# Where the inner rows of one batch are computed: after the attention, or beside the attention of the other batch

## The chip, the cores and the metric

One core of one Trainium2 chip runs the whole program. The metric is the device time of an execution in microseconds (us); several executions are timed, and one more is recorded by the hardware profiler. TensorE (PE) multiplies matrices and writes its sums into PSUM banks; ScalarE (ACT), VectorE (DVE) and GpSimd (POOL) read and write SBUF and PSUM; SyncE (SP) and ACT issue transfers between DRAM and SBUF on queues. Each engine runs its own list of instructions in order and waits on semaphores for the others.

## The reference

One transformer block in fp32, with batch 2, 1024 tokens, width 1024, 32 heads of 32 and an inner width of 2752. Cut to what matters:

```python
mod = (silu(c) @ wmod).reshape(2, 6, 1, -1)          # 1024 x 6144
sa, ca, ga, sb, cb, gb = ...                         # ga, gb kept away from zero
h = layernorm(x) * (1 + ca) + sa
qkv = clip(h @ Wqkv.T, -8, 8); q = layernorm(q); k = layernorm(k)
p = softmax(q k^T / sqrt(32) + alibi, causal)        # per head
x = x + ga * (p v) @ Wout.T
h = layernorm(x) * (1 + cb) + sb
x = x + gb * (((silu((h @ Wg.T) * ag) * ((h @ Wu.T) * au)) @ Wd.T) * ad)
```

## The kernel before

**Seven products.** Each large product is made by a scheme with seven products of half-size blocks where the plain one has eight (`SEVEN`, `seven`). It needs sums and differences of blocks of both operands; these are made ahead and kept in DRAM. For the down projection `down_weights` (L1203) loads a slice of Wd (four transfers on SP), makes four differences on POOL (L1212 to L1215) and stores them; `down_weights` is a generator with a `yield` after the differences and one after the stores.

**The inner rows.** The inner width 2752 is not a multiple of the blocks: 2560 columns go through the seven products, and 192 "inner rows" are left. They need the plain products, as three groups of 8 matmuls (128x128 by 128x256) for each pair of token tiles (b, j), with b = 0, 1 and j = 0 to 3: the first group is the gate of 128 rows, the second the up of the same, the third both for the last 64. `rest_rows` (L1373 and what follows) computes them: products (recorded at L762, the helper `matmul`), Silu on ACT (L1388, L1389), a product of gate and up on DVE (L1392), and a store. Their weights `restw` are loaded by `rest_weights` (L1360; transfers at L1370, a clearing at L1365).

**Stages.**
1. Modulation vectors and the projections of batch 0. `wmod` is fetched in pieces of 512 KB, `AHEAD` = 3 pieces ahead of the products that use them (L618), in a ring of 4 buffers.
2. Attention of both batches, about 379 to 1382 us. It is cut in 192 units (batch, 512 queries, 4 heads, 128 keys). A unit is: scores on PE into two PSUM tiles, exps on ACT (L1084), on the diagonal a mask on POOL (L1088), and two units later (`LAG` = 2) the product with the values (`av`). A sum over the exps goes to DVE or POOL (L1116), and a product with ones (`settle`) gives the row sums.
3. Beside the attention runs "dense work": first the projections of batch 1, with the slices of `down_weights` between them (a function `side` takes a step at two of three places), then `output(0, j)` for four tile pairs j, and `output(1, 0)` and `output(1, 1)`. An output is a seven-products group with the attention's Wout (24 us of PE), a gated residual sum on POOL (`xs`), a normalization, and four turns of four transposes each (through `ident`), whose tiles h2 are stored to DRAM (L1325).
4. The section after the attention ("rest section"), 1382 to 1557 us: `output(1, 2)` and `output(1, 3)`, all inner rows, and `second_batch`, which makes sums of both batches' tiles on DVE and POOL. Tiles h2 of earlier pairs are fetched from DRAM (`fetch`, L1548).
5. Gate and up products (L1817, from 1557 us) and the down products (L1942, from 2412 us) to the end.

**What sets the order.** Between the start of the attention and the end of the rest section PE's instructions are pinned to the order in which the program is written down. `together(att, dense, share)` decides it: attention yields an estimated time per unit, dense work yields its own, and dense work goes on while its sum is below `share` of the attention's. `share` gives dense work 16 + 370 over batch 0's attention and `DENSE1` = 136 more over that of batch 1. A `Todo` list holds small pieces (the turns) that an output takes up, one at each place between its seven products, if a fresh bank is there. Three PSUM banks serve dense work: two for the seven products (bank_331 and bank_332 in the trace), the third for turns and row sums.

In the rest section `with_turns` and a second `together` lay the inner rows between turns and output products. The inner rows stand in the order (0,0) (1,0) | (0,1) (1,1) | (0,2) (1,2) | (0,3) (1,3).

Of the kernel before, what the change touches and what calls it, by code (L numbers as in the profile page):

```python
# [480 lines left out]
def kernel(  # L481
# [234 lines left out]
    last_exp = [None]  # L716

# [157 lines left out]
    class Todo:  # L875
# [18 lines left out]
        def add(self, go):  # L894
            self.list.append(go)

        def run(self, n, all_=False):
            self.place()
            for _ in range(min(n, len(self.list))):
                if not all_ and not self.banks.fresh():  # L900
                    return
                self.list.pop(0)(self.banks.turn())
                yield TURN
# [124 lines left out]
    def attention(pools, adders, banks):  # L1028
# [22 lines left out]
        def scores(b, qb, k, jb):  # L1051
            qc, kc, _ = chunks[b, qb, k]
            y0 = max(qb * QB, jb * P)
            end = (qb + 1) * QB
            n = end - y0
            span = SPAN.get(k, QB)
            out_ = {}
            first = None

            for half in (1, 0):  # L1060
                sp = scp.tile([P, 2, QB], FP, tag=f"sc{half}", name=f"sc_{b}_{k}_{qb}_{jb}_{half}")
                p = prp.tile(
                    [P, 2, QB], FP, tag="p" if jb else f"p0{half}", name=f"p_{b}_{k}_{qb}_{jb}_{half}",
                    bufs=None if jb else 2,
                )
                for g in range(2):
                    r0 = (2 * half + g) * HD
                    ins = matmul(
                        sp[:, g, 0:n], kc[r0 : r0 + HD, ts(jb, P)], qc[r0 : r0 + HD, ds(y0 - qb * QB, n)],
                        start=True, stop=True,  # L1070
                    )
                    if first is None:
                        first = ins
                    else:
                        behind(ins, first)
                out_[half] = (sp, p)
            for half in range(2):
                sp, p = out_[half]
                for g in range(2):
                    h_ = 4 * k + 2 * half + g  # L1080
                    for y in range(y0 // span * span, end, span):
                        lo, hi = max(y, y0) - y0, y + span - y0
                        d = jb - y // P + {128: 7, 256: 6, 512: 4}[span]
                        last_exp[0] = nc.scalar.activation(  # L1084
                            p[:, g, lo:hi], sp[:, g, lo:hi], AF.Exp, bias=kw[:, d, h_ : h_ + 1]
                        )
                if jb * P >= qb * QB:
                    nc.gpsimd.affine_select(  # L1088
                        out=p[:, :, 0:P], in_=p[:, :, 0:P], pattern=[[0, 2], [1, P]],
                        compare_op=ALU.is_ge, fill=0.0, base=0, channel_multiplier=-1,  # L1090
                    )
            return [out_[half][1] for half in range(2)]
# [110 lines left out]
    def down_weights(i, pool):  # L1203


        s, c_ = i // 4, i % 4
# [5 lines left out]
        nc.gpsimd.tensor_sub(w[:, 0], w[:, 1], w[:, 0])  # L1212
# [28 lines left out]
    def operand(b, j, ap_):  # L1241
# [3 lines left out]
        for g in range(4):  # L1245
# [5 lines left out]
            q: ap_.tile(  # L1251
                [P, KC // 2, P], FP, tag=q, name=f"ao{q}_{b}_{j}",
                bufs=2 if q in ("A21", "A22") else None,
# [17 lines left out]
    def output(b, js, pools, banks, bt, todo, keep, made={}, q0=1):  # L1271
# [9 lines left out]
        for j in js:  # L1281
# [11 lines left out]
            def read(q, bank):  # L1293
# [5 lines left out]
                yg = partp.tile([P, 512], FP, tag=f"yg{n}", name=f"yg_{q}_{b}_{j}")  # L1299
                if q == "U6":  # L1300
                    nc.vector.tensor_mul(yg, ga[:, ts(n, HALF)], bank)
                else:
                    nc.vector.tensor_add(yg, part_t[MATE[q]], bank)
# [13 lines left out]
            for m in range(2):  # L1317
                for g in range(2):
# [10 lines left out]
                    todo.add(go)  # L1329

# [21 lines left out]
    LEAD, DENSE0, DENSE1 = 16.0, 370.0, 136.0  # L1352
# [7 lines left out]
    def rest_weights(pool, eng):  # L1360
# [10 lines left out]
        return w  # L1371

# [49 lines left out]
    with ExitStack() as st:  # L1422
        five = st.enter_context(tc.tile_pool(name="five", bufs=1, space=PSUM))
        wmr = st.enter_context(tc.tile_pool(name="wmr", bufs=4))
# [10 lines left out]
        AHEAD = 3  # L1435
# [60 lines left out]
    def dense_work():  # L1496
        yield from dense0
        with tc.tile_pool(name="wdsum", bufs=2) as dwp:
            steps = itertools.chain.from_iterable(down_weights(i, dwp) for i in range(4 * NSB))

            def side(n, e):

                at = 7 * n + e - 24
                if at >= 0 and at % 3 != 2:
                    next(steps, None)
# [9 lines left out]
            for n, k in (("oga", 1), ("tok", 4), ("opart", 1), ("osmall", 2), ("ao", 1))  # L1515
# [3 lines left out]
        bt = weights_b(wop, wout_t, "o", wt_dram[3])  # L1519
        out_args.extend((opools, banks, bt, Todo(banks), keep))  # L1520
        yield from output(0, range(NJ), *out_args, made)
# [18 lines left out]
    pair_pool = right["rest"] = pair_st.enter_context(tc.tile_pool(name="pair", bufs=1, side="right"))  # L1540
    rest_pool = rest_st.enter_context(tc.tile_pool(name="rest", bufs=1, side="right"))
# [15 lines left out]
    def with_turns(rows_):  # L1557

        together(rows_, todo.run(len(todo.list), True), lambda a: 0.16 * (a - 9.0))

    fetch(0, 0, nc.scalar)
    rest_w = rest_weights(rest_pool, nc.scalar)
    fetch(1, 0, nc.scalar)
    made = {(1, NJ // 2): operand(1, NJ // 2, opools[1])}
    fetch(0, 1)
    with_turns(rows((0, 0), (1, 0)))
    fetch(1, 1)

    def between():
        yield from rows((0, 1))  # L1570
# [4 lines left out]
        between(), output(1, range(NJ // 2, NJ), *out_args, made, 3), lambda a: 0.6 * OUT_US / 2 * a / 20.6  # L1575
# [5 lines left out]
    with_turns(rows((0, 2), (1, 2)))  # L1581
    second(2)
    alone(rows((0, 3), (1, 3)))
# [461 lines left out]
```

## Time and profile before

| what | us |
|---|---|
| median of 3 runs | 2912.99 |
| lowest and highest of them | 2908.82, 2913.18 |
| profiled execution, its own time | 2906.93 |
| its span in the profile | 2905.2 |
| granted clock of PE, mean | 0.976 |
| attention of batch 1 | 979 to 1381 |
| rest section | 1382 to 1557 |
| PE busy in 979 to 1381, of 402.00 | 347.49 |
| PE busy in 1382 to 1557, of 175.00 | 153.39 |

The profile lists for each engine the busy time, then the span in 40 equal slices, each a digit for the busy tenths. An fp32 matmul is two instructions in the trace, so a group of 8 products counts 16. The view of waits names for each engine the instruction that waited (engine, output tile, line), what released it, and the total, the number and the longest of such waits. The timeline gives start, duration, engine, line, operation and tiles, with the idle time before it in brackets.

### The profile page before, as it was taken

How to read it: one execution, taken by the hardware profiler on the slowest of the kernel's cores; microseconds unless marked ns; L12 is line 12 of the kernel's file. 1: busy time of each engine (PE TensorE's matmuls, PEld its weight loads, DVE VectorE, ACT ScalarE, POOL GpSimd, SP SyncE). 2: the span in 40 equal slices, each digit the busy share in tenths (PEclk: the TensorE clock that was granted, in tenths of full speed). 3: DMA queues.
4: the chain of work that ended last, by engine and by line, in shares of the span. 5: the costliest groups of instructions: out<-in, count | busy, mean ns of one | idle time of the engine just before them, and what ended most of it. 6: DMA issues, size and time to landing. Idle time of an engine off the chain costs nothing. (4 is left out here: it accounts for less than half of the span.)

```text
span 2905.2 us, 29905 instructions
## 1 busy us (share of the span) xinstructions
PE 2723.2 (94%) x10271; PEld 1336.5 (46%) x10271; DVE 1448.4 (50%) x2285; ACT 685.7 (24%) x1523; POOL 1294.0 (45%) x1270
## 2 busy tenths in 40 slices
PE   6999898999999898988799999999999998999998
PEld 2444333333333232222565444444444446888776
DVE  5765522566643456666464353453535346444442
ACT  1322232344444456555021011010101100000000
POOL 3311146523454665656357455464744541222343
PEclk9999999999999899999899999999999999999999
DMA  9877797563461555432777667585766659555542
GB/s 341 301 254 282 295 312 223 174 217 114 173 178 62 210 171 150 147 107 86 222 234 252 217 213 244 169 278 167 263 199 195 233 165 289 158 152 145 157 145 81
DMA packets 377573, 579.14 MB, mean 199 GB/s; under 512 B 21590, under 2 KB 278712, under 8 KB 366276
## 3 DMA queue, kind: packets, MB, share of 16 engines
q1 hardware_dynamic: 359768, 554.54, 58.8%
q10 hardware_dynamic: 17644, 22.59, 2.5%
q8 instruction: 84, 1.38, 0.2%
q14 instruction: 77, 0.63, 0.1%
HBM read 411.89 MB, written 165.17 MB: 199 GB/s over the span
## 5 line engine op out<-in xcount | busy, mean ns | idle before, releaser
L1084 ACT ACTIVATE p<-sc,kw 128x128 f32<-128x128 f32 (+3 forms) x1024 | 421.7, 513 | 382.5 <-PE sc L762 365.4
L762 PE MATMUL bank<-wT,a 128*128 128x512 f32 x768 | 360.0, 612 | 14.0 <-DVE raw L983 7.1
L1116 POOL TENSOR_TENSOR p<-p,p 128x1024 f32<-128x1024 f32 (+3 forms) x128 | 259.3, 2026 | 243.6 <-PE av L762 211.5
L1116 DVE TENSOR_TENSOR p<-p,p 128x1024 f32<-128x1024 f32 (+3 forms) x192 | 243.8, 1280 | 190.4 <-POOL p L1088 132.8
L762 PE MATMUL bank<-wB,a 128*128 128x512 f32 x576 | 266.0, 606 | 2.1 <-DVE raw L981 1.3
L762 PE MATMUL sc<-cq,ck 32*128 32x512 f32 (+3 forms) x1536 | 193.5, 543 | 53.0 <-ACT p L1084 52.7
L762 PEld LDWEIGHTS bank<-wT,a 128*128 128x128 f32 x768 | 142.6, 195 | 192.7 <-issue 174.6
L1088 POOL TENSOR_SCALAR_AFFINE_SELECT p<-p 128x256 f32<-128x256 f32 x256 | 139.2, 560 | 125.9 <-ACT p L1084 123.3
L762 PE MATMUL av<-p,cv 128*32 128x512 f32 (+3 forms) x1536 | 173.9, 514 | 16.6 <-POOL p L1088 16.6
L762 PEld LDWEIGHTS bank<-wB,a 128*128 128x128 f32 x576 | 105.1, 191 | 149.5 <-issue 128.8
L762 PEld LDWEIGHTS sc<-cq,ck 32*128 32x128 f32 x1536 | 64.9, 187 | 190.3 <-ACT p L1084 101.6
L1817 PE MATMUL gy<-bt,sig 128*128 128x512 f32 x280 | 132.5, 596 | 10.8 <-DMA bt<-bop_B 6.2
L1817 PE MATMUL gx<-bt,sig 128*128 128x512 f32 x280 | 131.6, 592 | 0.0
L1817 PE MATMUL uy<-bt,siu 128*128 128x512 f32 x280 | 131.6, 592 | 0.0
L1817 PE MATMUL ux<-bt,siu 128*128 128x512 f32 x280 | 131.6, 592 | 0.0
L762 PEld LDWEIGHTS av<-p,cv 128*32 128x32 f32 x1536 | 34.4, 110 | 139.1 <-issue 85.3
L1817 PEld LDWEIGHTS gy<-bt,sig 128*128 128x128 f32 x280 | 52.4, 190 | 81.1 <-issue 71.5
L1817 PEld LDWEIGHTS ux<-bt,siu 128*128 128x128 f32 x280 | 53.2, 190 | 66.9 <-issue 64.3
L1817 PEld LDWEIGHTS gx<-bt,sig 128*128 128x128 f32 x280 | 53.2, 190 | 66.9 <-issue 66.6
L1817 PEld LDWEIGHTS uy<-bt,siu 128*128 128x128 f32 x280 | 53.2, 190 | 66.9 <-issue 66.2
L762 PE MATMUL rest<-hl,restw 128*128 128x256 f32 x288 | 67.7, 394 | 15.7 <-DMA x<-xr 15.7
L1817 PE MATMUL gx<-bt,wgS 128*128 128x512 f32 x160 | 75.2, 592 | 0.0
(416 smaller groups left out, 4481.2 us busy)
## 6 DMA issues: line engine op xcount, KB each, us to landing
bt<-bop_T SPq DMA_DIRECT2D x140, 512.0 KB
bt<-bop_B SPq DMA_DIRECT2D x99, 512.0 KB
a<-hop SPq DMA_DIRECT2D x20, 1792.0 KB
wm<-in_L_wmod_dram SPq DMA_DIRECT2D x48, 512.0 KB
wB<-in_L_attn_Wqkv_dram SPq DMA_DIRECT2D x21, 1024.0 KB
aq_S<-act_S SPq DMA_DIRECT2D x16, 1280.0 KB
qk<-qs SPq DMA_DIRECT2D x16, 1024.0 KB
act_S<-asS SPq DMA_DIRECT2D x30, 512.0 KB
```

The lines of the kernel that those rows point to most:

```text
L762: return in_order(nc.tensor.matmul(*args, **kw_))
L1084: last_exp[0] = nc.scalar.activation(p[:, g, lo:hi], sp[:, g, lo:hi], AF.Exp, bias=kw[:, d, h_ : h_ + 1])
L1088: nc.gpsimd.affine_select(out=p[:, :, 0:P], in_=p[:, :, 0:P], pattern=[[0, 2], [1, P]], compare_op=ALU.is_ge, fill=0.0, base=0, channel_mu ...
L1116: adders[b](half, jb).tensor_add(dst, dst, ps[half][:, :, 0:n])
L1817: nc.tensor.matmul(ps.rearrange("p (j t) -> p j t", j=NJ), ins[mat][qa][:, c2, :], bt[:, :, c2, :], start=(q in ("P1", "P2", "P5") and c2 ...
```

## The change

- `Todo` entries get a time; an entry with no time needs no bank.
- `rest_pieces` (new) puts batch 0's inner rows in the to-do list of `output(0, j)`, three PE pieces a pair, so that they run inside the attention of batch 1. ACT empties the bank with scaled copies and takes exp(−gate), DVE builds gate / (1 + exp(−gate)) × up (Silu written out), SP stores. The rows (0, j) leave the rest section.
- The inner rows' weights are loaded on SP's queue ahead of `output(0, ·)`, not on ACT's queue after the attention.
- `down_weights` yields between its loads and its differences; these stand behind the latest mask. `side` takes a step at every place.
- `AHEAD` is 5 and its ring has 6 buffers. `DENSE1` is 177; pacing constants in the rest section change.
- Memory: gated products of an output are written into the tiles of its parts, and `tok`, `osmall` and two operand tiles have one buffer less. `output(1, 2)`'s operand gets a pool of its own, and `output(1, 3)`'s is made early.

```diff
@@ Todo @@
-        def add(self, go):
-            self.list.append(go)
+        def add(self, go, us=TURN):
+            self.list.append((go, us))
         def run(self, n, all_=False):
             self.place()
-            for _ in range(min(n, len(self.list))):
+            while n and self.list:
+                go, us = self.list[0]
+                if us is None:
+                    go()
+                    self.list.pop(0)
+                    continue
                 if not all_ and not self.banks.fresh():
                     return
-                self.list.pop(0)(self.banks.turn())
-                yield TURN
+                self.list.pop(0)
+                go(self.banks.turn())
+                n -= 1
+                yield us
@@ scores @@
-                    nc.gpsimd.affine_select(
+                    last_mask[0] = nc.gpsimd.affine_select(
@@ down_weights @@
                 nc.sync.dma_start(w[:, 2 * kh + n], ...)
-        nc.gpsimd.tensor_sub(w[:, 0], w[:, 1], w[:, 0])
+        yield
+        behind(nc.gpsimd.tensor_sub(w[:, 0], w[:, 1], w[:, 0]), last_mask[0])
@@ operand @@
-                bufs=2 if q in ("A21", "A22") else None,
@@ output @@
-                yg = partp.tile([P, 512], FP, tag=f"yg{n}", ...)
+                yg = part_t[MATE.get(q, "P5")]
...
-                    nc.vector.tensor_add(yg, part_t[MATE[q]], bank)
+                    nc.vector.tensor_add(yg, yg, bank)
...
                     todo.add(go)
+            if rest is not None:
+                rest_pieces(b, j, todo, h2, *rest)
@@ constants @@
-    LEAD, DENSE0, DENSE1 = 16.0, 370.0, 136.0
+    LEAD, DENSE0, DENSE1 = 16.0, 370.0, 177.0
...
-        AHEAD = 3
+        AHEAD = 5
...
-                at = 7 * n + e - 24
-                if at >= 0 and at % 3 != 2:
+                if 7 * n + e >= 24:
                     next(steps, None)
@@ rest_pieces, new @@
+        def scaled(dst, ps, vec, r, rows_):
+            ib = vec + 4 * NSB + r
+            nc.scalar.activation(dst, ps, AF.Identity, scale=vt[rows_, ib : ib + 1])
+        def product(w, bank):
+            ps = bank[:, 0:256]
+            for k in range(KC):
+                matmul(ps, w[:, k, :], hl[:, k, :], start=(k == 0), stop=(k == KC - 1))
+            return ps
+        def gate(ps, r, lo, hi):
...
+            scaled(g[hi], ps[lo], R_AG, r, lo)
+            nc.scalar.activation(e[hi], g[hi], AF.Exp, scale=-1.0)
...
+        def act(r, hi, n):
+            g, e = tiles[r]
+            nc.vector.tensor_scalar(e[hi], e[hi], FAR, 1.0, ALU.min, ALU.add)
+            nc.vector.reciprocal(e[hi], e[hi])
+            nc.vector.tensor_mul(g[hi], g[hi], e[hi])
+            nc.vector.tensor_mul(g[hi], g[hi], urow[hi])
+            nc.sync.dma_start(rest_dram[r][0:n, b, j], g[hi].rearrange("p (h t) -> p h t", h=2))
...
+        todo.add(lambda bank: gate(product(rest_w[0], bank), 0, every, every), 3.5)
+        todo.add(lambda bank: up(product(rest_w[1], bank), 0, every), 3.5)
+        todo.add(lambda: act(0, every, P), None)
+        todo.add(last, 3.5)
+        todo.add(lambda: act(1, hi, n1), None)
@@ dense_work @@
+        rwp = ost.enter_context(tc.tile_pool(name="restw", bufs=1))
         out_args.extend((opools, banks, bt, Todo(banks), keep))
-        yield from output(0, range(NJ), *out_args, made)
+        right["w"] = rest_weights(rwp, nc.sync)
+        yield from output(0, range(NJ), *out_args, made, rest=(right["w"], rwp))
@@ rest section @@
-        together(rows_, todo.run(len(todo.list), True), lambda a: 0.16 * (a - 9.0))
+        together(rows_, todo.run(len(todo.list), True), lambda a: 0.3 * (a - 3.0))
-    fetch(0, 0, nc.scalar)
-    rest_w = rest_weights(rest_pool, nc.scalar)
+    rest_w = right["w"]
     fetch(1, 0, nc.scalar)
-    made = {(1, NJ // 2): operand(1, NJ // 2, opools[1])}
+    fetch(0, 0, nc.scalar)
+    made = {(1, NJ // 2): operand(1, NJ // 2, opools[1], wide)}
+    made[1, NJ // 2 + 1] = operand(1, NJ // 2 + 1, opools[1])
     fetch(0, 1)
-    with_turns(rows((0, 0), (1, 0)))
+    with_turns(rows((1, 0)))
     fetch(1, 1)
     def between():
-        yield from rows((0, 1))
         second(0)
         yield from rows((1, 1))
     together(
-        between(), output(1, range(NJ // 2, NJ), *out_args, made, 3), lambda a: 0.6 * OUT_US / 2 * a / 20.6
+        between(), output(1, range(NJ // 2, NJ), *out_args, made, 3), lambda a: 0.6 * OUT_US / 2 * a / 10.3
     )
...
-    with_turns(rows((0, 2), (1, 2)))
+    with_turns(rows((1, 2)))
     second(2)
-    alone(rows((0, 3), (1, 3)))
+    alone(rows((1, 3)))
```

## The prediction

> **What bounds the kernel now.** I read the shares and the forty slices first, then PE's waits over the whole span, then the same waits stage by stage.
>
> ```profile
> PE 2723.2 (94%) x10271; PEld 1336.5 (46%) x10271; DVE 1448.4 (50%) x2285; ACT 685.7 (24%) x1523; POOL 1294.0 (45%) x1270
> ...
> PE   6999898999999898988799999999999998999998
> ...
> PEclk9999999999999899999899999999999999999999
> ```
>
> PE is busy 94% of the span; no other engine passes 50%. The slices that dip (counted from 0, 72.6 us each) are 4 and 6, the projections and the first attention, then 13 to 19, batch 1's attention and the section after it. The end moves only by PE's work and PE's idle time. The waits of the whole span:
>
> ```profile
> PE sc L762 <- ACT p L1084: 52.7, 52, 3.8
> PE av L762 <- POOL p L1088: 16.6, 9, 4.7
> PE rest L762 <- DMA x<-xr: 15.7, 1, 15.7
> ...
> PE more L618 <- DMA wm<-in_L_wmod_dram: 6.8, 2, 3.4
> ```
>
> Columns: total us, times, longest. The change speaks to each of these four. Of the 52.7 us for exps (scores find their bank not yet read by ScalarE), 45.2 lie in the window 979 to 1381 us, batch 1's attention:
>
> ```profile
> 979.00:1381.00 402.00, 347.49 (x2029) 112.86 (x2032) 236.88 (x344) 228.38 (x553) 248.92 (x232) 0.93 0.42 129
> ```
>
> Of 402 us, PE is busy 347.5 and idle 54.5; ScalarE works 228, POOL 249, so every other engine has room on the average.
>
> **Part 1, the modulation weights fetched 5 ahead, not 3.** Two waits of 3.4 us, at 306 and 342 us: the fetch was late. Two more buffers issue it two pieces earlier, while PE has other work. −6 (0 if the queue, not the buffer, was late; −9 with the cold products behind them).
>
> **Part 2, down-weight subtractions behind masks.** POOL's row at 440.7 us shows the harm:
>
> ```profile
> 440.73 0.72 POOL L1213 TENSOR_TENSOR wdr<-wdr 128x256 f32<-128x256 f32 x1 [6.85 <-DMA wdr<-in_L_ffn_Wd_dram]
> ```
>
> POOL runs in order; it stands 6.85 us for a slice still in flight, and the masks (L1088) queued behind stand too, so attention-value products wait. And the PE timeline shows the price:
>
> ```profile
> 458.86 1.00 PE L762 MATMUL av<-p,cv 128*32 128x128 f32 x8 [4.67 <-POOL p L1088]
> 460.10 6.00 PE L762 MATMUL bank<-wT,a 128*128 128x512 f32 x8 [0.23 <-DVE raw L983]
> ```
>
> After the 4.67 us wait, eight products take 6.00 us where 3.60 is usual. Between 379 and 979 us these waits are 12.6 us in 5. Now a slice's loads are issued a step ahead of its subtractions, which stand behind a mask: eight of 0.72 us, 5.8 us, between two masks, hidden because a value product comes two units after its scores. Should a slice still be late there, the next masks and the operand sums of POOL queue behind it as before. −12.6, and about −2.4 for the cold products: −15. Bounds −3 (most waits merely move, as subtractions are now spread over more units) and −22 (every cold row).
>
> **Part 3, twelve products beside attention.** Per tile pair three pieces of 8 products (128x256) go into batch 1's attention. After the attention six groups of the same shape took 20.7 us, 3.45 a piece, so 12 × 3.45 = 41.4 us of PE time enter. They would be free if they fell into idle time, but this is scattered. Here is one unit without dense work:
>
> ```profile
> 1299.82 1.14 PE L762 MATMUL sc<-cq,ck 32*128 32x512 f32 x8
> 1300.89 1.06 PE L762 MATMUL av<-p,cv 128*32 128x512 f32 x8
> 1303.50 0.71 PE L762 MATMUL sc<-cq,ck 32*128 32x512 f32 x4 [1.55 <-ACT p L1084]
> ```
>
> From score to score 3.68 us pass: scores 1.07, 0.14, the exps 2.42, 0.05. PE works 2.1 and idles 1.55. A piece put here makes the work 5.5: it fills 1.55 and adds 1.9. Where dense work already fills the unit, it adds all of 3.45. I summed the 96 score-to-score stretches, each as the larger of PE work and exp cycle. Before: 372.7 (work 312.9, short 59.8). After, by the new order of instructions, in which 10 of 12 pieces are alone in their stretch: 400.2. That is +27.5; following the queues in sequence gave +33.4. I take **+30**. Bounds: 0 (all in idle time) and +41.4.
>
> What goes with a piece: ScalarE empties the bank (by its Silu row, 0.47) and takes one exp per gate: six such activations a pair, 24 × 0.4 = 10 us of ScalarE on 228. VectorE gets about 6 us a pair, 24 on 237 (reciprocal 0.95 for 128 columns). Both have room. The cover is that dense work follows; if a group lands ahead of four exps that PE waits for, it costs its 0.4 to 0.9. Stores go on SP's queue, small. The third bank, held 3.45 + 0.5 longer, serves turns and row sums as well.
>
> A rule speaks to this. The row first: granted clock 0.93 over these 402 us, in which the 41 waits for exps sum to 45.2 us, 1.1 each, longest 3.8. The Trainium skill, "TensorE: Matmul & The Clock Gate", section "Part 1: The HAM clock gate", has the clock fall only after an idle window of about 3.4 us. By it filling gaps of 1.55 us returns no clock, and +30 stays; by the row a fuller PE might give some of it back, which would make it +26 or so.
>
> **Part 4, the section after attention.** From 1381.6 to the first gate product at 1556.8 are 175.2 us. What goes: 12 pieces, 41.4, and this wait on the PE timeline:
>
> ```profile
> 1390.76 3.60 PE L762 MATMUL bank<-wT_o,aoA 128*128 128x512 f32 x8
> 1410.05 2.47 PE L762 MATMUL rest<-hl,restw 128*128 128x256 f32 x5 [15.69 <-DMA x<-xr]
> ```
>
> It is labelled by another transfer, but the rest weights end their issue on ScalarE's queue only at 1409.5. Now SP issues them before batch 1's attention, 1.5 MB behind the output weights, where the transfers' share is 0.42 to 0.57, and POOL's clearing of 0.95 goes with them: nothing there, and −15.7 here. Together −57.1. What is late next, now that batch 0's rows no longer cover it:
> - the inner row of (1,0) waits for its own operand (fetch issued at 1392.8; landing about 1396): +2;
> - the two turns of tile 2 behind it need the residual sum, the normalization and ScalarE's root, queued behind the gate's activation with its table loads of 1.28: about +8, with banks +2;
> - (1,1)'s rows stand at PE's head before output (1,2), and their operand goes through DRAM (SP store issued 1442.2, fetch 1449.0 in the old trace, 6.8 apart, and some 5 until it has landed): +12. PE runs in order, so output (1,2) with all behind it waits too, though its own operands are there;
> - the tail: normalization from last product to normalized row took 9 us, with 3.45 of products left as cover: 5.5, and 3 for turns and evacuation: +8.5;
> - less the 4.8 us in which tile turns wait now, which these take in.
> Sum 2 + 8 + 2 + 12 + 8.5 − 4.8 = +28. Net **−29**: the section lasts about 146 us. Bounds −15 (+42: each wait half as long again) and −45 (+12).
>
> The row again: the 15.69 wait is followed by 48 instructions in 12.39 us where 10.35 is usual, so each long wait costs some 2 more.
>
> **Part 5, memory saved.** Gate products are written into the parts' tiles, tok and small tiles lose a buffer, A21 and A22 are single. Each may make the next pair wait for POOL's sum; output products last 24 us a pair, POOL's work in it about 10, so 0 (up to +4). Pacing constants change the place of pieces, not their number: 0. Gate and down stages (1557 to the end) keep their order on PE: 0.
>
> **Sum**: −6 −15 +30 −29 = −20. On the profiled execution 2906.9 (span 2905.2 and 1.7 around it) gives 2887. The median of the runs shown, 2913.0, is 6 above that execution, so the forecast is **2893**.
>
> **Rivals.**
> - *B, more is won.* Round trip and turns cost 12, not 28, and the fuller PE keeps its clock: −29 becomes −45, +30 becomes +26: −6 −15 +26 −45 = −40, 2873. For it: POOL (75.9 of 175) and VectorE (94.7) are half idle after attention. Against: the round trip is serial.
> - *C, the waits take the place.* The new waits after attention cost 45, not 28: −12 there, and −6 −15 +30 −12 = −3: 2910, no change; with part 2 at its bound of −3 it is +9, 2922. For it: the 15.7 us of the old weights' wait and batch 0's rows covered exactly those chains.
> - *D, slower.* One mechanism: attention's cycle takes more than a piece's own time. ScalarE's emptying (0.47 and an exp, 0.9) stands ahead of the exps, and the third bank, held meanwhile, puts off a tile's turns with their 1.4 of emptying (1.37 for four), so a piece costs 3.45 + 0.9 + 1.4 = 5.8: 12 × 5.8 = 70, and −6 −15 −29 +70 = +20: 2933. It decides from (50 + 5.8) / 12 = 4.6 us a piece. For it: sc waits of ACT are the largest wait already. Against: ScalarE is idle 174 of 402 us.
> - *The change does not do what it says*: pieces could find no fresh bank and fall out to the end of each pair. The pinned order shows them between scores, so this is small and within C.
>
> **Chances.** A (the forecast) 0.46, since each of its terms is read from a row; B 0.20; C 0.16; D 0.18, since the tail of the attention's cycle is the one cost that no row shows. Measurement of this kernel can tell about 0.2% (5.8 us) from no change. A and B and a little of C are faster: 0.68; same 0.12 (C); slower 0.20 (D, and C's end). Range 2872 to 2922: B's middle, A's and C's whole, the near part of D.
>
> **What would show it.** Right: no wait of `rest` on weights; attention of batch 1 about 430 us, not 402; mask waits before 979 us under 3; no wm waits; the first gate product near 1537 (1557 − 20), with waits of `rest` on hl and of turns on xn after attention. Wrong: attention of batch 1 over 450 us (D) or under 415 (B); or new waits over 42 us behind it (C).

## The result, and the profile after

The changed kernel takes 2912.28 us (median of 12 runs), the kernel before 2910.16 (12 runs). The ratio is 1.0005, with a 95% interval of 0.9997 to 1.0013: no change, where 20 us less were forecast. That is not because nothing happened: stage by stage, large gains and large losses cancel. The stages are bounded by instructions that both traces have (the first score, the first score of batch 1, the last value product, the first gate and the first down product).

| stage, us | before | after | difference | forecast |
|---|---|---|---|---|
| to the first score | 378.1 | 359.3 | −18.8 | −6 |
| batch 0's attention | 600.9 | 587.3 | −13.6 | −15 |
| of it units 8 to 80 | 460.4 | 433.9 | −26.5 | |
| of it units 88 to 96 | 48.0 | 60.9 | +12.9 | 0 |
| batch 1's attention | 401.5 | 444.2 | +42.7 | +30 |
| section after the attention | 176.3 | 167.8 | −8.5 | −29 |
| gate and up | 855.9 | 851.5 | −4.4 | 0 |
| down | 492.5 | 497.1 | +4.6 | 0 |

The page of the changed kernel, PE's shares and slices:

```profile
PE 2704.0 (93%) x10271; PEld 1335.8 (46%) x10271; DVE 1471.4 (51%) x2309; ACT 692.0 (24%) x1539; POOL 1286.9 (44%) x1270
...
PE   7999999999997888888598999999999998999998
```

PE has the same 10271 instructions and is busy 19 us less, yet the span is 2 us longer. Slices 1 to 11 are full now (4 and 6 were not), slice 12 has a new dip, and slice 19, the section after attention, has fallen from 7 to 5. The waits of PE over the whole span show what changed:

```profile
PE sc L763 <- ACT p L1093: 44.8, 48, 3.7
PE bank L766 <- DVE xn L747: 26.2, 5, 12.2
PE rest L763 <- DMA hl<-h: 23.1, 2, 14.7
PE bank L763 <- DVE aoS L1273: 16.6, 1, 16.6
...
PE av L763 <- POOL p L1097: 2.9, 1, 2.9
PE more L618 <- DMA wm<-in_L_wmod_dram: 2.6, 1, 2.6
```

Mask waits are down from 16.6 to 2.9 us, waits for modulation weights from 6.8 to 2.6, the wait for inner weights is gone. Three rows are new: turns that wait for a normalized row (xn), inner rows that wait for a tile from DRAM (hl), and one of 16.6 us for the operand of the first output (aoS). By stages, with the same columns as in the prediction:

```profile
947.00:1391.00 444.00, 383.64 (x2216) 147.14 (x2212) 267.36 (x378) 238.36 (x577) 240.20 (x232) 0.95 0.39 121
1391.00:1558.00 167.00, 120.34 (x395) 74.92 (x388) 90.58 (x171) 19.69 (x29) 81.00 (x70) 0.85 0.75 240
```

Batch 1's attention has 36 us more of PE work and 6 us more idle time. The section after it has 34 us less work, is only 8.5 us shorter, and its granted clock is 0.85, not 0.94. Part of its PE timeline:

```profile
1414.59 5.92 PE L763 MATMUL rest<-hl,restw 128*128 128x256 f32 x16 [8.35 <-DMA hl<-h]
1427.58 1.11 PE L766 MATMUL bank<-ident,xn 128*128 128x128 f32 x4 [7.07 <-DVE xn L747]
1428.49 5.74 PE L763 MATMUL rest<-hl,restw 128*128 128x256 f32 x16
1434.06 0.60 PE L766 MATMUL bank<-ident,xn 128*128 128x128 f32 x4
1434.50 3.62 PE L763 MATMUL rest<-hl,restw 128*128 128x256 f32 x16
```

Two waits, and the piece behind each takes 5.9 and 5.7 us where the third takes 3.6. (The Trainium skill, "TensorE: Matmul & The Clock Gate", section "Part 1: The HAM clock gate", has the clock fall after an idle window of about 3.4 us and return after as much work. Both waits are longer than that, so these rows agree with it.)

Short waits do not agree with it. In batch 1's attention of the kernel before, the granted clock is 0.50 from 1092.8 to 1096.2 us, and the only waits of PE in the 12 us ahead are the two shown here, of 0.78 and 0.24 us:

```profile
1090.20 0.91 PE L762 MATMUL sc<-cq,ck 32*128 32x384 f32 x4 [0.78 <-ACT p L1084]
1091.35 0.91 PE L762 MATMUL sc<-cq,ck 32*128 32x384 f32 x4 [0.24 <-ACT p L1084]
1092.19 3.21 PE L762 MATMUL bank<-wT_o,aoA 128*128 128x512 f32 x4
```

```profile
1092.80:1096.20 3.40, 3.40 (x16) 1.00 (x18) 0.90 (x2) 1.61 (x5) 3.32 (x6) 0.50 0.16 64
```

So the clock of this stage, 0.93 before, does not come from long waits alone.

### The profile page after: what moved, and what is told of

It reads as the page before. It is cut to its first block, busy times and chain, and to the rows that moved or that the text cites. A ratio compares the mean times of both kernels' runs of the same rounds, so it can differ in the third digit from the quotient of the medians.

```text
span 2907.2 us, 29960 instructions
## 1 busy us (share of the span) xinstructions
PE 2704.0 (93%) x10271; PEld 1335.8 (46%) x10271; DVE 1471.4 (51%) x2309; ACT 692.0 (24%) x1539; POOL 1286.9 (44%) x1270
## 4 chain that ended last, share of the span: by engine, by line
PE 47%; DMA 5%; DVE 4%; issue 4%; POOL 3%; ACT 1%; SPq 0%; ACTq 0%; POOLq 0%; DVEq 0%
PE ux L1881 8%; PE gx L1881 8%; PE dx L2006 7%; PE gy L1881 6%; PE uy L1881 6%; PE dy L2006 5%; PE bank L763 3%; PE sc L763 2%; ACT p L1093 1%; PE av L763 1%; DMA bt<-bop_B 1%; POOL xr L1316 1%; DMA bop_T<-inner_T 1%; DMA aoA<-ao 1%; DMA wuA<-in_L_ffn_Wu_dram 1%
## 5 line engine op out<-in xcount | busy, mean ns | idle before, releaser
L1097 POOL TENSOR_SCALAR_AFFINE_SELECT p<-p 128x256 f32<-128x256 f32 x256 | 127.1, 508 | 215.4 <-ACT p L1093 210.3
L763 PEld LDWEIGHTS av<-p,cv 128*32 128x32 f32 x1536 | 32.5, 109 | 117.9 <-issue 80.6
L763 PE MATMUL bank<-wB_o,aoA 128*128 128x512 f32 x128 | 66.2, 650 | 16.6 <-DVE aoS L1273 16.6
L1881 PE MATMUL ux<-bt,wuS 128*128 128x512 f32 x160 | 75.2, 592 | 0.0
```

The lines of the kernel that those rows point to most:

```text
L763: return in_order(nc.tensor.matmul(*args, **kw_))
L1097: last_mask[0] = nc.gpsimd.affine_select(out=p[:, :, 0:P], in_=p[:, :, 0:P], pattern=[[0, 2], [1, P]], compare_op=ALU.is_ge, fill=0.0, bas ...
L1881: nc.tensor.matmul(ps.rearrange("p (j t) -> p j t", j=NJ), ins[mat][qa][:, c2, :], bt[:, :, c2, :], start=(q in ("P1", "P2", "P5") and c2 ...
```

## The experiments

Each run was compared with the kernel before on the same chip. Stage times are those of one profiled execution, bounded as in the table above. The same stage differs by some us between executions: over the seven kernels with the weights 3 ahead, the first score lies between 378.0 and 383.3 us.

### The two early parts alone, and both (e1, e2, e5)

e1 is the kernel before with this:

```diff
-        AHEAD = 3
+        AHEAD = 5
-        wmr = st.enter_context(tc.tile_pool(name="wmr", bufs=4))
+        wmr = st.enter_context(tc.tile_pool(name="wmr", bufs=6))
```

> The kernel before with one part of the change: modulation weights fetched 5 pieces ahead, in a ring of 6. In the changed kernel the attention starts 18.8 us earlier than before (359.3 for 378.1), three times what the forecast gave this part. Theory: all of it is this part, two long waits gone and the modulation products in longer runs between the projections' products (fewer changes between the two forms). Then this kernel takes about 2905 - 19 = 2887 in its span, the attention starts at 359 to 361, and all behind it is as before. Rival: only the 6 us of named waits are this part's, the rest comes from elsewhere in the change; attention starts near 372 and the time is 2899.

Measured: ratio 0.9952 (0.9928 to 0.9976), some 14 us. The first score is at 367.9. Over all kernels the seven with 3 ahead have it at 378.0 to 383.3 (mean 379.7), the thirteen with 5 ahead at 359.3 to 367.9 (mean 364.4): 15 us. So the gain is this part's, and 18.8 was a lucky pair of executions. The named waits fall by 4 us only; PE's busy time falls from 341.7 to 332.3 us with the same 1062 instructions. The reason is in the timeline. First two stretches of the kernel before, then the changed one:

```profile
244.86 1.06 PE L618 MATMUL more<-wm,sc 128*32 128x512 f32 x8
```

```profile
255.28 1.05 PE L618 MATMUL more<-wm,sc 128*32 128x512 f32 x4
256.27 1.12 PE L762 MATMUL bank<-wB,a 128*128 128x512 f32 x2
257.32 1.05 PE L618 MATMUL more<-wm,sc 128*32 128x512 f32 x4
```

```profile
246.24 1.91 PE L618 MATMUL more<-wm,sc 128*32 128x512 f32 x12
```

Four modulation instructions between projection products take 1.05 us, eight in a row 1.06 and twelve 1.91. Eight cost what four cost because they run side by side: in the run at 244.86 us the first four start within 0.02 us of each other and each lasts 0.62 us, and the other four follow in the same way. In runs of four, only two run at a time. With more pieces loaded, the products stand in longer runs: before, 24 runs, of which 19 have four instructions; 5 ahead, 13 runs, of which 4 have four.

e2 is the kernel before with the slices' part:

```diff
+        yield
-        nc.gpsimd.tensor_sub(w[:, 0], w[:, 1], w[:, 0])
+        behind(nc.gpsimd.tensor_sub(w[:, 0], w[:, 1], w[:, 0]), last_mask[0])
...
-                at = 7 * n + e - 24
-                if at >= 0 and at % 3 != 2:
+                if 7 * n + e >= 24:
```

> The kernel before with one part of the change: down-weight slices with their differences behind a mask and a step at every place. In the changed kernel units 8 to 24 and 72 to 80 of the attention are 28 us shorter, and one wait of 16.6 us is new where the first output's operand is late. Theory: both are this part's; the slices now end at 887 us and not at 527, and hold the memory that the operand (0,0) needs, so it is loaded only when PE is about to need it. Then units 8 to 80 take some 28 us less, the wait for the operand sum is there again (10 to 17 us), and the time is 2905 - 28 + 13 = 2890. Rival: the late operand comes from the early inner weights on SP ahead of it (3.9 us of issue); then the wait is under 6 us here and the time about 2880.

Measured: ratio 0.9920 (0.9892 to 0.9947). Units 8 to 80 take 432.6, 27.8 less; units 88 to 96 take 54.2, 6.2 more, with a wait of 11.2 us for the output's weights. The theory holds in its sizes, though what PE waits for here is named as the weights and not the operand; e8 below tests whether the slices cause it. Between the traces of before and of the changed kernel, PE's idle time in these units falls from 32 to 14 us. The other 9 us are busy time at the same 1968 instructions: the granted clock is 0.99 and not 0.97, so fewer products run slowly.

e5 has both parts and nothing else of the change.

> The kernel before with both parts that won alone: weights fetched 5 ahead, and slices behind masks; no products beside attention, no early inner weights, no memory saved. Theory: the two lie in different stages and add up: ratios 0.9952 x 0.992 = 0.987 of before, some 37 us. That is more than the changed kernel and more than the kernel without pieces gained, because this one has not the saved memory. Rival: the memory saved costs nothing, and the kernel without pieces (2880.7 in its profile) shows the real sum, so this one, which lacks the early inner weights, is slower than it by 12 to 16: ratio 0.995 or more.

Measured: ratio 0.9862 (0.9846 to 0.9879), 40 us less. The parts add up (0.9952 × 0.9920 = 0.9872), and two parts of the change alone are far better than all of it. The rival falls.

### The pieces beside attention (e3, e4)

e3 is the changed kernel with the pieces put back:

```diff
-        yield from output(0, range(NJ), *out_args, made, rest=(right["w"], rwp))
+        yield from output(0, range(NJ), *out_args, made)
...
-    with_turns(rows((1, 0)))
+    with_turns(rows((0, 0), (1, 0)))
```

and so for the other rows, `DENSE1` and the pacing.

> The changed kernel without its twelve products beside attention: batch 0's inner rows are back in the section after the attention with Silu, pacing constants of that section and DENSE1 as before; the weights still come early, and the other parts stay. Theory: the pieces cost 43 us beside attention (more than the 41.4 of their products), and after the attention they cover the waits of 8, 7, 15 and 12 us for tiles fetched and normalized, so they are nearly free there. Batch 1's attention is back at 402, the section after it takes 155 to 163, and the span is 2907 - 43 + (0 to -8) = about 2856 to 2864. Rival: the pieces are worth their place, and this kernel gains only what the early weights give, the section after attention takes 175 + 0 and more since waits stay, 2875 or over.

Measured: ratio 0.9952 (0.9932 to 0.9973), 15 us better than the changed kernel by ratios, 26.5 in the profiled spans. Batch 1's attention takes 418.7, so against this kernel the pieces cost 444.2 − 418.7 = 25.5 us there, not 43: they do fill 16 us of idle time. The section after attention takes 163.6 *with* the 41 us of products that the changed kernel has moved away, and 167.8 without them. After the attention these products were free: they covered waits, and kept the clock at 0.99. Other kernels repeat both stages: 440.9 to 443.6 with the pieces (e4, e7, e13, e15, e18), and 159.5 to 161.1 in the section with all inner rows and two of the three weights early (e14, e16, e17). But the profiled execution of e3 is the fastest of its seven, 11 us under their median, so the 26.5 of the spans is too much for a usual execution; which stage differs in the others is not known.

And 418.7 is not the 401.5 of before: 17 us that no theory of mine had. They are idle time: PE stands for 75 us of this stage in e3, and for 54 in the kernel before.

e4 keeps the pieces' products and leaves out their activations and VectorE's work:

```diff
-            scaled(g[hi], ps[lo], R_AG, r, lo)
-            nc.scalar.activation(e[hi], g[hi], AF.Exp, scale=-1.0)
...
-            nc.vector.tensor_mul(g[hi], g[hi], urow[hi])
-            nc.sync.dma_start(rest_dram[r][0:n, b, j], g[hi].rearrange("p (h t) -> p h t", h=2))
+            nc.sync.dma_start(rest_dram[r][0:n, b, j], h2[hi, r])
```

> The changed kernel, with the twelve pieces' products run but their sums thrown away: no activation of ScalarE, no work of VectorE, and the store writes other data (so batch 0's inner rows are wrong). Theory: a piece costs its own PE time, and holds a bank for turns; emptying it costs nothing, so batch 1's attention is 440 to 446 us as in the changed kernel, and the time 2903 to 2908. Rival D of the forecast: emptying by ScalarE ahead of the exps and the bank held for it cost 0.9 to 2.3 a piece, so 11 to 28 us go: 2879 to 2896.

Measured: ratio 0.9987 (0.9970 to 1.0004); batch 1's attention 440.9, 3.3 less than with everything. Rival D falls: emptying the bank and the Silu written out cost 0.3 us a piece. So the cost is PE's own time, less the idle time that it fills.

### What the saved memory costs (e6, e9 to e12)

e6 is the kernel before with the four memory savings alone.

> The kernel before with only the memory savings: gated products written into the parts' tiles, tok 3, osmall 1, the two operand tiles single. Theory: these cost the 17 us by which batch 1's attention is longer in the kernel without pieces (418.7 for 402): each pair's parts wait for POOL's sum of the pair before and the turns for a late normalization, so batch 1's attention takes 412 to 420 here and the time is 2918 to 2925. Rival (the forecast: 0, up to +4): the 17 us come from the late operand, which shifts the dense work; then the attention of batch 1 is 402 to 406 and the time 2905 to 2909.

Measured: ratio 1.0095 (1.0078 to 1.0112), 28 us slower. Batch 1's attention takes 421.7, and units 88 to 96 take 58.5 with this on PE:

```profile
956.81 3.75 PE L762 MATMUL bank<-wB_o,aoA 128*128 128x512 f32 x4 [15.25 <-DMA wB_o<-in_L_attn_Wout_dram]
```

Then each saving by itself. The operand tiles:

```diff
                 [P, KC // 2, P], FP, tag=q, name=f"ao{q}_{b}_{j}",
-                bufs=2 if q in ("A21", "A22") else None,
```

> The kernel before with one of the four memory savings: the operand tiles A21 and A22 single. Theory: this is the costly one of the four, which together made batch 1's attention 421.7 us, not 402, and held the first output back by 15 us. A single tile can only be loaded when the pair before has made its last product with it; VectorE, in order, then waits up to 11 us for that load and keeps sums and turns of the attention waiting. Batch 1's attention takes 415 to 420, the time 2920 to 2930. Rival: another of the four; then 402 to 406 and 2905 to 2911.

The gated products:

```diff
-                yg = partp.tile([P, 512], FP, tag=f"yg{n}", name=f"yg_{q}_{b}_{j}")
+                yg = part_t[MATE.get(q, "P5")]
```

> The kernel before with one of the four memory savings: gated products written into the tiles of the parts. Theory (operand tiles cost it): nothing, 402 to 406 in batch 1's attention, 2905 to 2911. Rival: ScalarE's copy of the next pair's part waits for POOL's sum of this pair, a bank stays full and PE waits: 410 to 420, 2915 to 2930.

The residual rows, `("tok", 4)` to `("tok", 3)`:

> The kernel before with one of the four memory savings: three tok buffers, not four. Theory (operand tiles cost it): the residual rows of the next pair are loaded one tile later, well ahead of their sum; 402 to 406 in batch 1's attention, 2905 to 2911. Rival: the second residual tile comes late and the normalization with it: 410 to 420.

The small tiles, `("osmall", 2)` to `("osmall", 1)`:

> The kernel before with one of the four memory savings: one set of the small tiles of a normalization, not two. Theory (operand tiles cost it): 402 to 406 in batch 1's attention, 2905 to 2911. Rival: a normalization waits for the one before it: 406 to 415. Either way the 15 us by which the first output came late may belong here or to any of the four, by where the pool of the output's weights comes to lie; the wait for the weights wB_o, 3.9 before and 15.2 with all four, tells.

| run | ratio | 95% interval | batch 1's attention | units 88 to 96 |
|---|---|---|---|---|
| e9, A21 and A22 single | 1.0050 | 1.0034 to 1.0066 | 415.2 | 47.7 |
| e10, gated products in the parts' tiles | 1.0003 | 0.9989 to 1.0017 | 392.6 | 46.9 |
| e11, three tok buffers | 0.9992 | 0.9980 to 1.0004 | 398.4 | 47.9 |
| e12, one set of small tiles | 0.9994 | 0.9979 to 1.0008 | 397.9 | 47.0 |

The single operand tiles cost some 14 us, the other three nothing. Batch 1's attention in e9, PE's waits and then two of VectorE's:

```profile
PE sc L762 <- ACT p L1084: 43.5, 40, 3.7
PE av L762 <- POOL p L1088: 11.9, 5, 5.1
```

```profile
DVE aoA L1260 <- DMA aoA<-ao: 7.6, 1, 7.6
DVE aoA L1260 <- DMA cv<-v: 4.0, 1, 4.0
```

VectorE stands 11.6 us for operand tiles that can only be loaded late (3.7 before), and value products wait 11.9 us for masks and sums (4.0 before). That the one leads to the other is argued from the order in the queues, not shown by itself. In the changed kernel neither shows: VectorE's wait for operand tiles is 4.0 us in this stage and PE's for masks 2.9, where e3, without the pieces, has 16.8 and 14.0. So there the pieces stand partly in idle time that the single tiles make, and the prices of the two do not simply add; no run has the pieces with double operand tiles. And no single saving makes the first output late: the 15 us need more than one.

### Another order after the attention (e7)

```diff
-    with_turns(rows((1, 0)))
-    fetch(1, 1)
     def between():
+        yield from rows((1, 0))
+        fetch(1, 1)
         second(0)
+        yield 8.0
         yield from rows((1, 1))
...
-        ... lambda a: 0.6 * OUT_US / 2 * a / 10.3
+        ... lambda a: 14.0 + 1.8 * a
```

> The changed kernel, with another order after attention: output (1,2) follows at once, the turns of (1,1) and the rows of (1,0) stand between its products, the rows of (1,1) come some 8 us of products after their fetch is written down, and the last of them cover the last normalization. Same work. Theory: the section after attention gained nothing from 41 us of products less because the chain of stores, fetches and normalizations sets it (waits of 8.4, 7.1, 14.7, 12.2 us); with products put in their place 25 to 40 us go, the section takes 128 to 143 and the span is about 2867 to 2882. Rival: the section is set by something earlier (the last row sums' reciprocals, through DRAM, to operand (1,2)), and the waits only move to the start of output (1,2): 5 to 10 us go.

Measured: ratio 0.9977 (0.9966 to 0.9988); the section takes 161.5, 6.3 less. The waits for hl are gone, and output (1, 2), now first, waits 23.1 us for its own operand, which needs the last row sums through DRAM. The rival was right. My reading is that several chains of about the same length start at the attention's end, and that PE needs work that depends on none of them. Batch 0's inner rows were just that.

### Why the first output is late, and a faster kernel (e8, e13 to e18)

e8 is e5 with a slice in two steps, so that the slices end at 792 us:

```diff
             nc.sync.dma_start(wd_dram[o][:, s, :, ts(c_, P)], w[:, r])
-        yield
```

> As the kernel with the two parts that won alone, but a slice takes two steps and not three (its stores go with the next slice's loads), so that the slices end at two thirds of their stretch, near 770 us and not 887, and free the memory of the first output's operand and weights. Theory: the wait of 11 us there goes, 7 to 13 us less than the kernel with the two parts. Rival: the denser slices bring mask waits back (as before, 12 us), and nothing is won.

Measured: ratio 0.9855 (0.9838 to 0.9871). In the profile units 88 to 96 are back at 46.9 (54.9 in e5), but the ratio is not told apart from e5's. e13 makes the same edit in the changed kernel.

> The changed kernel, with slices in two steps each and not three, so that they end near 770 us. Theory: the slices' tiles hold the memory, so the first output's operand is loaded in time, the wait of 16.6 us goes and units 88 to 96 take 48 us, not 61: 9 to 13 us less, span near 2896. Rival: the memory savings' new places in memory make it wait (as 15.2 us in the kernel with these alone); then the wait stays over 10 us and the span is 2903 or more.

Measured: ratio 0.9993 (0.9983 to 1.0003); the wait stays, 15.9 us. So there the slices aren't the cause. e14 adds to e8 two of the three inner weights loaded early, paid for with savings that cost nothing (e10 and e11):

```diff
+        rwp = ost.enter_context(tc.tile_pool(name="restw", bufs=1))
         out_args.extend((opools, banks, bt, Todo(banks), keep))
+        right["w"] = rest_weights(rwp, nc.sync)
...
-    rest_w = rest_weights(rest_pool, nc.scalar)
+    rest_w = rest_weights(rest_pool, nc.scalar, right["w"])
```

> The kernel with the parts that won (weights 5 ahead, slices behind masks in two steps each), with two of the three inner weights loaded on SP before the outputs, in memory freed by the two savings that cost nothing (gated products in the parts' tiles, tok 3); operand tiles stay double, no products beside attention, the third inner weight is loaded after attention as before. Theory: the wait of 15.7 us for inner weights goes, less what the chains of tiles and normalization then show (the kernel without pieces: 12.7 us less in this section): 8 to 13 us under the kernel without early weights (2858.7 in its span, ratio 0.9855), so 2846 to 2851, ratio 0.981 to 0.983. Rival: the wait only changes its name (tile (0,0) is fetched, the third weight late): less than 5 us.

Measured: ratio 0.9835 (0.9813 to 0.9858). The section after attention takes 161.1, not 175.7, but the late operand is back (15.9 us) and takes it away again. SP's queue in e14 and in e8, the loads of that operand:

```profile
906.16 0.43 SPq L1247 DMA_DIRECT2D rb<-rec  x1
906.64 0.44 SPq L1261 DMA_DIRECT2D aoA<-ao  x1
```

```profile
797.36 0.43 SPq L1247 DMA_DIRECT2D rb<-rec  x1
797.83 2.82 SPq L1261 DMA_DIRECT2D aoA<-ao  x2
```

A hundred microseconds apart, with nothing in the code that orders them otherwise. What differs is the memory: the savings in the pools opened ahead of the operand's pool move it, in e14 by 8 KB a partition. e15 and e16 are e13 and e14 with the inner weights' pool opened ahead of the outputs' pools, which moves the operand's pool up again:

```diff
+        rwp = ost.enter_context(tc.tile_pool(name="restw", bufs=1))
         gap_, tkp, partp, osm, aop = [
...
-        rwp = ost.enter_context(tc.tile_pool(name="restw", bufs=1))
```

> The changed kernel with slices in two steps, and with the pool of the inner weights opened before the outputs' other pools and not behind them. Theory: the operand's pool lies above the projections' tiles again, so the wait of 15.9 us for the operand sum goes: span 9 to 13 us under the 2909.9 without this, about 2898, ratio about 0.995. Rival: the place is not it; wait and time stay.

> The kernel with the winning parts and two inner weights early, with the pool of the inner weights opened before the outputs' other pools: 8 KB that put the operand's pool back to where it was in the kernel before. Theory: the wait of 15.9 us goes, the attention of batch 1 begins at 936 and not 951, and the gain of the early weights (14.6 us in the section after attention) is left: span 2844 to 2849, ratio 0.979 to 0.981. Rival: the place is not it; 2859 as without this.

Measured: in both the wait for the operand goes (4.2 and 3.9 us are left, as before; units 88 to 96 take 47.3 and 47.7). But e15 has a ratio of 1.0033 (1.0024 to 1.0043) and e16 of 0.9839 (0.9816 to 0.9863). The time is lost at the gate stage (871.6 and 872.0 us, 20 and 15 more than in e13 and e14), as this row of e16 shows:

```profile
1516.59 3.78 PE L1821 MATMUL gx<-bt,sig 128*128 128x512 f32 x4 [17.43 <-POOL sig L1686]
```

There POOL makes 28 sums of the gate weights (wgS, wuS) ahead of the first stage's own (sig); in e14 `sig` comes first. So both forecasts were right about the operand and wrong about the time. The last two runs put the pool between: directly below the operand's.

```diff
-            for n, k in (("oga", 1), ("tok", 3), ("opart", 1), ("osmall", 2), ("ao", 1))
+            for n, k in (("oga", 1), ("tok", 3), ("opart", 1), ("osmall", 2), ("restw", 1), ("ao", 1))
```

> The kernel with the winning parts and two inner weights early, the inner weights' pool now directly below the operand's pool. Theory: the operand is still in time (its place is the same as in the run before), and the gate stage's first tiles are no longer held by the inner weights, so neither wait shows: batch 1's attention begins near 936, the first gate product at 1492 to 1495, the span is 2841 to 2846, ratio 0.977 to 0.980. Rival: any early weights cost the gate stage what they save; 2855 or more.

> The changed kernel with slices in two steps and the inner weights' pool directly below the operand's pool. Theory: the wait of 15.9 us for the first operand goes, as in the run before, and the gate stage starts without a new wait: span 2896 to 2900, ratio 0.995 to 0.997, which is what the twelve products and the single operand tiles leave of the gains. Rival: as in the run before, over 2910.

Measured: e17 has 2848.95 us and a ratio of 0.9787 (0.9767 to 0.9807), which is within its forecast, and the fastest of all; e18, the changed kernel with both repairs, has 0.9980 (0.9966 to 0.9994), a smaller gain than its forecast and hardly told apart from e13. Units 88 to 96 take 48.5 and 51.6, the gate stage 858.1 and 851.8. The long wait for the operand is gone; 5.5 and 8.0 us are left for the output's weights (3.9 before). The wait for `sig` is gone too. From e14 to e16 and e17, and from e13 to e15 and e18, the edits move nothing but the place of this pool, so that place caused both waits. Which tiles overlap is not in the profile; that they are those of the last projections, and at the other end the first gate weights on the inner weights, is inferred. One row of e16 fits the second: POOL's first sum for wgS waits 5.94 us for PE's inner rows.

```profile
1493.09 1.40 POOL L1674 TENSOR_TENSOR wgS<-wgS,wgA 128x256 f32<-128x256 f32 x2 [5.94 <-PE rest L763]
```

The section after attention in e17:

```profile
1341.00:1501.00 160.00, 153.23 (x596) 105.38 (x589) 87.14 (x180) 22.91 (x36) 75.49 (x66) 0.99 0.81 256
```

All inner rows are in it, PE is busy 153 of 160 us, and the clock is 0.99.

## Why the prediction was wrong

The forecast was −20; the measured difference is nothing. In the profiled stages nearly the whole miss lies in part 4 (−8.5 for −29). The three stages ahead of it come to +10.3 where I had +9, but by luck: the first is 13 us better than forecast and batch 1's attention 13 us worse. By its steps:

- **Part 1 (−6): right in direction, mis-sized.** 15 us (e1 and the mean over all kernels). I counted the waits and not that pieces loaded earlier let the modulation products stand in longer runs, where up to eight instructions take the time of four.
- **Part 2 (−15): half right.** Units 8 to 80 gain 27.8 (e2): idle time fell by 18 us where I had 12.6, and slow products by 9 where I had one group of 2.4. But I did not ask what the slices, spread over 300 us more, keep occupied: in e2 the first output's weights come 11 us late.
- **Part 3 (+30): near in size, but not tested as forecast.** Against e3 the pieces cost 25.5 us in the attention, within 5 us of the sum over 96 stretches. But the sum was made on the stage before, where PE idles 54 us; in e3 it idles 75. Against the kernel before, the stage is 42.7 us longer, over my upper bound of 41.4, with part 5 in it. So the nearness may be luck. The rule that I cited, by which only an idle window of about 3.4 us lowers the clock, did not hold in this stage: the row at 1092.8 us shows half the clock after waits of 0.78 us at most. The stage's granted clock rose from 0.93 to 0.95. That ScalarE's emptying is nearly free is shown by e4.
- **Part 4 (−29): failed.** The waits have the names I gave them: 8.4 for tile (1,0) (I said 2), 8.7 for the turns behind it (10), 14.7 for (1,1) (12), 15.0 in the tail (8.5), 46.7 in all for 32.5. The sum is then −41.4 − 15.7 + 40.9 + 7.7 = −8.5, where 40.9 is 46.7 less the 5.8 us of waits that were there besides the one for weights, and 7.7 is what remains. Most of it is slow products, which I mentioned and left out of the sum: behind the four long waits the next rows take 9.7 us more than usual, and behind the two longest of before 3.8. This is rival C at its own place; that its total came true as well is the same luck. What I had not seen is that the early weights gain 12.7 us here without the pieces moved (e3: 163.6), so moving them made this section longer. The step that failed is the +28 for the waits that batch 0's rows had covered: with the slow products it is 48.6, more than the 41.4 of products that were moved away.
- **Part 5 (0, up to +4): failed.** "Each may make the next pair wait for POOL's sum" looked at the wrong queue. The single operand tiles cost 14 us (e9), and the four savings 28 with the late first output (e6). Counted from before to e3 this is 17 us of batch 1's attention; the 13 us in units 88 to 96, which stood in no part of the forecast, come from the place of the pools (e15).

The sum of the profiled stages, with e3 as the step between, though another order of steps would divide batch 1's attention differently: −18.8 to the first score, −26.5 by the slices and −12.7 by the early weights, against +12.9 for the late operand, +17.2 for the saved memory in batch 1's attention, and +25.5 beside and +4.2 behind the attention for the pieces; with +0.2 in gate and down this is +2.0, the difference of the spans. The pieces are dear twice: they need the memory, and they leave a place where they cost nothing.

## What to carry to other kernels

Work that depends on nothing is worth most where several chains start at once; before moving it into a busier stage, ask what covers the waits that it leaves. Buffers given up to make room are part of the price, and so is the place where the pools behind them come to lie: try each saving alone, and look at when the first load of each pool is issued. A change of several parts is best measured part by part; here two of them were worth 1.4%, and all together nothing.

## What the runs showed of the hardware that was not expected

Products with narrow weights (128x32, those of the modulation) run side by side on PE, and how many do depends on the order in which they are issued. Up to the first score PE's busy time is 343.8 us in the mean of the seven kernels with 3 pieces ahead and 332.3 in the thirteen with 5, at the same 1062 instructions. From the start of the last projection product before a run of modulation instructions to the start of the second one behind it, a run of four adds 1.18 us to two usual steps of 0.43, a run of eight 1.19, of twelve 2.04 and of twenty 2.90. That is 0.85 for each group of up to eight, and about 0.33 for going over to the other kind and back. With 3 ahead there are 27 such groups in 24 runs, with 5 ahead 20 in 13: an estimate of 7 × 0.85 + 11 × 0.33 = 9.6 us from these rows, where e1 has 9.4. So about 6 of them come from products side by side and the rest from fewer changes.
